# Batch norm rows over 128 partitions instead of 97 in a four-layer scan, convolution and attention kernel

## The chip, the cores and the metric

The kernel runs on one core of a Trainium2 chip. The metric is the device time of one execution in microseconds (us). TensorE is PE in the profile, VectorE is DVE, ScalarE is ACT, GpSimd is POOL, and SyncE is SP; SP computes nothing here and issues every DMA, in order, on one queue.

## What is computed

The input is x, of shape (4, 96, 64, 64): four images with 96 channels. Four layers follow each other. Layer 0 is a selective scan in four directions over the 4096 positions of an image, and it holds most of the work. Layer 1 is a block of three convolutions with batch norms (96 to 576 channels, 3x3 depthwise, 576 to 96). Layer 2 is a Fourier attention and a quantised feed-forward net; layer 3 is a linear attention and another such net. What bears on the change are two batch norms that follow a matrix product directly:

```python
# layer 1: h has 576 channels
scale = g * rsqrt(v + EPS);  shift = b - m * g * rsqrt(v + EPS)
h = relu(einsum('oc,bchw->bohw', w1, x) * scale + shift)
...
# layer 2: h has 192 channels
h = einsum('bnc,hc->bnh', x, w1)
h = relu((h - mean) * (gamma / sqrt(var + EPS)) + beta)
```

Scale and shift depend on weights alone. So the scale can be multiplied into the columns of the weight matrix, and the shift can become one more row of it, which is multiplied by a row of ones.

## The kernel before

**The folded matrices.** The kernel holds w1 as a matrix of 128 rows (input channels) by 576 columns, of which 96 rows are weights and row 96 is the shift; the tile wa1 of layer 2 is the same with 192 columns. The image has a channel 96 that is constant one. The generator `later_weights` (L324) builds them, once in the whole program. It loads each of the four batch norm vectors g, b, m, v as a row that is repeated over the partitions: `load_row` (L161) issues one DMA on SP whose source is the vector in DRAM, broadcast over as many partitions as the target has. The targets have C + 1 = 97 partitions (L332, L333 for layer 1, 576 columns; L382, L383 for layer 2, 192 columns). Then `rsqrt` (L167, L168, two ACT instructions) and three DVE instructions (L361, L363, L365, and L409, L410, L412) make scale and shift on all 97 partitions. Rows 0 to 95 of the scale multiply the weights (L367, L413), and row 96 of the shift is copied into row 96 of the matrix (L368, L415).

**The scan.** The long part of the program is `scans` (L1225). It walks through 1536 units, each one a block of 128 partitions by 1024 positions. For each unit ACT computes the decay (L1279), POOL multiplies the input by B (L1272), DVE runs the scan (L1286), DVE or POOL multiplies by C (L1301), and PE sums with a constant matrix (L1324). ACT is one unit ahead of the scan and POOL two. The inputs scan_d, scan_g, scan_B, scan_C are fetched by SP (L1257), each as a 512 KB load that is broadcast over partitions.

**What sets the order.** The instruction order of every engine is fixed when the program is built: the scan runs in a manual schedule, and after each unit a planner (`advance`) puts in steps of the other layers, which are written as generators that yield (engine, estimated time). The first stage that the planner serves is `weights` (L1219): `later_weights` beside `group_norm` of images 1 to 3 (L509). A group norm loads an image in eight chunks of 192 KB (`fetch_image`, L502) and takes the statistics of each chunk on DVE (`bn_stats`, L516). Both generators start together. So SP's queue holds, in this order: the loads of w1, w2 and other weights (L327), two of wout (L330, L331), the four rows of 576 columns and two of 96 columns (L162), then the first three chunks of image 1 (L502), then scan inputs (L1257), then the next chunks.

SP's DMAs take turns on eight semaphore lanes. A DMA waits at the head of SP's queue until the DMA eight before it has landed. The third chunk of image 1 is eight behind the first row, the next scan_g is eight behind the second, and so on.

The four layer-2 rows (L383) come about 110 us later in the same way, between the layer's other weights and two loads of rdid (L385, L386).

Of the kernel before, what the change touches and what calls it, by code (L numbers as in the profile page):

```python
# [27 lines left out]
B, C, H, W = 4, 96, 64, 64  # L28
L = H * W
K, NS, R, DI = 4, 16, 6, 192  # L30
NE = R + 2 * NS
HID, NT1 = 576, 5
# [64 lines left out]
def hybrid_kernel(ctx: ExitStack, tc: tile.TileContext, a: dict):  # L97
# [63 lines left out]
    def load_row(out, name):  # L161
        load(out, a["rows"][:, ROW[name]].partition_broadcast(out.shape[0]))  # L162
        return out
# [32 lines left out]
    def big(name):  # L196
        if last_room and turns(thirds) == "last":
            return last_room[0].tile([128, 6144], F32, name=name, tag="big", bufs=1)
        return bp.tile([128, 6144], F32, name=name, tag="big", bufs=2)
# [86 lines left out]
    def scratch(t):  # L286

        at = 0

        def take(parts, *shape):  # L290
            nonlocal at
            n = int(np.prod(shape))
            at += n
            out = t[:parts, at - n : at]
            return out if len(shape) == 1 else out.rearrange("p (a b) -> p a b", b=shape[1])

        return take
# [26 lines left out]
    def later_weights():  # L324
# [3 lines left out]
        take = scratch(big("weights"))  # L328
        wo_a, wo_b = take(128, C), take(64, C)
        load(wo_a, a["wout_t"][0:128])  # L330
        load(wo_b, a["wout_t"][128:DI])  # L331
        s1, t1 = take(C + 1, HID), take(C + 1, HID)  # L332
        g1, b1, m1, v1 = (load_row(take(C + 1, HID), n) for n in ("g1", "b1", "m1", "v1"))  # L333
        g2r, v2r = load_row(take(128, C), "g2"), load_row(take(128, C), "v2")
        yield wait(4)
        yield pe(1.0, 1)
# [40 lines left out]
        take = scratch(big("weights"))  # L377
# [1 line left out]
        load(pre, a["pre"])  # L379
        w1t = take(C, DI)  # L380
        load(w1t, a["wa1_t"])
        sa, ta = take(C + 1, DI), take(C + 1, DI)  # L382
        ga, ba, ma, va = (load_row(take(C + 1, DI), n) for n in ("bn1_g", "bn1_b", "bn1_m", "bn1_v"))  # L383
        g, v = load_row(take(128, C), "bn2_g"), load_row(take(128, C), "bn2_v")
        load_row(rdid[0:64], "rd")  # L385
        load_row(rdid[64:128], "id")  # L386
# [3 lines left out]
        n = 2 * NG  # L390
# [35 lines left out]
        take = scratch(big("weights"))  # L426
# [789 lines left out]
    def plan():  # L1216

        stats = (group_norm(b, arriving(b)) for b in range(1, B))
        out = [Stage("weights", 2, later_weights(), *stats)] + front(1) + front(2)  # L1219
        out += middle(0) + layers_2_and_3(0) + front(3)  # L1220
        for b in (1, 2):
            out += middle(b) + layers_2_and_3(b)
        return out
# [417 lines left out]
```

## Time and profile before

| what | value |
|---|---|
| time, median of 3 runs | 6271.16 us (6259.06 to 6287.62) |
| the profiled execution | 6292.35 us, of which the span is 6290.6 us |
| busy: PE, DVE, ACT, POOL | 74%, 86%, 61%, 81% of the span |
| DMA | 1078.10 MB, 171 GB/s on average |
| L1286, DVE scan, mean of one | 2.28 to 2.35 us by form |
| L1301, DVE product, mean of one | 1.225 us |
| L1272, POOL product, mean of one | 2.373 us |
| L516, DVE statistics of one chunk, median | 0.672 us |
| granted PE clock, mean | 0.837 |

Times in the profile are from the start of the span. A row of the timeline gives the start and the length in us, the engine, the line, the operation, what is written and read, and how many instructions were merged; in brackets stands how long the engine had been idle before and which event ended that. SPq rows are DMA issues on SP's queue. Their length is the time that the issue kept the queue, not that of the transfer.

### The profile page before, as it was taken

To read this page: it belongs to the slowest core of one execution; us is meant where nothing else is said; L and a number is where in the kernel's file an instruction comes from. 1 tells how busy PE (TensorE), PEld (TensorE's weight loads), DVE (VectorE), ACT (ScalarE), POOL (GpSimd) and SP (SyncE) were. 2 spreads that over 40 slices of the span, in tenths; PEclk is the share of its full clock that TensorE was granted. 3 is DMA by queue.
4 is the path that set the end of the run, shared out by engine and by line. 5 is a ranking of instruction groups with operands and counts; after the bars stand their busy time and mean duration, and the time that the engine had idled before them with its cause. 6 is when DMAs were issued, how large, how long until landed. Compare 5 with 4: busy or idle time off the path is not lost. (4 is left out here: it accounts for less than half of the span.)

```text
span 6290.6 us, 78721 instructions
## 1 busy us (share of the span) xinstructions
PE 4637.2 (74%) x27628; PEld 1718.8 (27%) x27628; DVE 5400.7 (86%) x3627; ACT 3837.2 (61%) x6056; POOL 5073.3 (81%) x2183
## 2 busy tenths in 40 slices
PE   6632867755887776686568887767888677778998
PEld 2100212211222542121112236321222542112283
DVE  4979898999999889989999998898999998899045
ACT  5743776764664576767545656767666567665334
POOL 4856878889999888888899998898999888899000
PEclk9855978877998888788679988778999888788999
DMA  5654565667644554456776446447754454674201
GB/s 184 215 159 139 188 203 186 215 212 231 205 155 144 179 181 140 139 192 194 226 228 188 157 147 202 154 156 220 228 162 156 165 176 156 188 223 139 72 15 37
DMA packets 424720, 1078.10 MB, mean 171 GB/s; under 512 B 79258, under 2 KB 81024, under 8 KB 423172
## 3 DMA queue, kind: packets, MB, share of 16 engines
q1 hardware_dynamic: 424324, 1073.06, 53.2%
q8 instruction: 220, 3.60, 0.2%
q14 instruction: 176, 1.44, 0.1%
HBM read 856.64 MB, written 220.66 MB: 171 GB/s over the span
## 5 line engine op out<-in xcount | busy, mean ns | idle before, releaser
L1272 POOL TENSOR_TENSOR scan_w<-scan_g,scan_B 128x1024 f32<-128x1024 f32 x1536 | 3606.6, 2373 | 452.8 <-PE ps_y L1324 358.3
L1279 ACT ACTIVATE ps_da<-scan_d,aneg 128x1024 f32<-128x1024 f32 x1536 | 1715.5, 1117 | 533.5 <-DVE scan_w L1286 273.6
L1301 POOL TENSOR_TENSOR scan_w<-scan_w,scan_C 128x1024 f32<-128x1024 f32 x640 | 1516.3, 2369 | 285.9 <-ACT state L1298 175.6
L1286 DVE TENSOR_TENSOR_SCAN ps_da<-ps_da,state,scan_w 128x1024 f32<-128x1024 f32 x672 | 1575.9, 2345 | 197.9 <-ACT ps_da L1279 175.1
L1324 PE MATMUL ps_y<-scan_w,cst 128*32 128x512 f32 x6144 | 1005.4, 733 | 561.6 <-ACT yt L1338 207.4
L1301 DVE TENSOR_TENSOR scan_w<-ps_da,scan_C 128x1024 f32<-128x1024 f32 x896 | 1097.3, 1225 | 71.6 <-DMA scan_C<-bc 3.6
L1286 DVE TENSOR_TENSOR_SCAN scan_w<-ps_da,state,scan_w 128x1024 f32<-128x1024 f32 x480 | 1123.4, 2340 | 38.8 <-ACT ps_da L1279 33.4
L1286 DVE TENSOR_TENSOR_SCAN ps_da<-ps_da,scan_w 128x1024 f32<-128x1024 f32 x224 | 511.9, 2285 | 86.3 <-ACT ps_da L1279 67.0
L1324 PEld LDWEIGHTS ps_y<-scan_w,cst 128*32 128x32 f32 x6144 | 148.4, 118 | 1215.6 <-issue 633.3
L1298 ACT COPY state<-ps_da 128x1 f32<-128x1 f32 x672 | 107.0, 159 | 603.4 <-DVE scan_w L1301 601.5
L1286 DVE TENSOR_TENSOR_SCAN scan_w<-ps_da,scan_w 128x1024 f32<-128x1024 f32 x160 | 364.8, 2280 | 23.9 <-ACT ps_da L1279 17.4
L827 PE MATMUL ps_mm<-h,wd 128*32 128x512 f32 x3168 | 366.5, 593 | 8.1 <-ACT r L167 7.0
L565 PE MATMUL ps_mm<-xp,taps 128*128 128x512 f32 x576 | 289.8, 646 | 62.3 <-ACT xp L545 31.0
L804 PE MATMUL ps_mm<-wd,w 128*32 128x512 f32 x2008 | 253.6, 616 | 20.7 <-ACT h L808 8.7
L616 PE MATMUL ps_mm<-xd,dtw 128*128 128x512 f32 x256 | 169.8, 756 | 99.6 <-ACT z L638 58.3
L999 PE MATMUL ps_mm<-wa,xp 128*64 128x96 f32 x1728 | 135.0, 319 | 99.4 <-DVE d L1004 80.5
L886 PE MATMUL ps_mm<-r,cst 128*128 128x512 f32 x220 | 152.0, 779 | 55.4 <-ACT acc L909 19.5
L625 ACT ACTIVATE z<-ps_mm 128x512 f32<-128x512 f32 x192 | 114.2, 595 | 127.9 <-PE ps_mm L620 62.1
L631 DVE SCALAR_TENSOR_TENSOR ps_mm<-ps_mm,z 128x512 f32<-128x512 f32 x192 | 131.7, 686 | 69.9 <-ACT z L629 69.0
L670 PE MATMUL ps_mm<-ya,cst 128*64 128x512 f32 x192 | 182.9, 1042 | 7.7 <-ACT acc L909 7.7
L1298 ACT COPY state<-scan_w 128x1 f32<-128x1 f32 x480 | 89.8, 187 | 152.1 <-DVE scan_w L1286 151.0
L808 ACT ACTIVATE h<-ps_mm 128x512 f32<-128x512 f32 x265 | 153.5, 595 | 46.0 <-PE ps_mm L804 43.7
(348 smaller groups left out, 6662.4 us busy)
## 6 DMA issues: line engine op xcount, KB each, us to landing
scan_g<-du SPq DMA_DIRECT2D x384, 512.0 KB, 5.1
scan_d<-delta SPq DMA_DIRECT2D x384, 512.0 KB, 6.0
scan_B<-bc SPq DMA_DIRECT2D x256, 512.0 KB, 5.0
scan_C<-bc SPq DMA_DIRECT2D x256, 512.0 KB, 5.4
y<-yt SPq DMA_DIRECT2D x384, 128.0 KB, 2.5
du<-g SPq DMA_DIRECT2D x128, 256.0 KB, 2.4
delta<-z SPq DMA_DIRECT2D x128, 256.0 KB, 2.7
tab<-in_etab SPq DMA_DIRECT2D x112, 256.0 KB, 4.3
```

The lines of the kernel that those rows point to most:

```text
L565: mm(p, lhsT=taps[:, t, 0:128], rhs=window(t, c + e), start=t == 0, stop=t == 8)
L616: mm(p, lhsT=dtw[:, o + 2 * third, 0:128], rhs=xd, start=True, stop=True)
L670: mm(split(p[:64]), lhsT=const("two")[:, :64], rhs=t[:, :L].rearrange("p (w h) -> p h w", h=H)[:, c * RPC : (c + 1) * RPC, :], start=True, ...
L804: mm(p[32 * n : 32 * n + 32], lhsT=w1[:, 32 * g : 32 * g + 32], rhs=xin[:, n : n + 15 : 2, 1 : W + 1], start=True, stop=True)
L808: act(h[:, :, 1 : W + 1], split(p), AF.Relu)
L827: mm(p[32 * n : 32 * n + 32], lhsT=held["wd"][:, groups[i], o, dx, :], rhs=here[i][:, :, dx : dx + W], start=dx == 0, stop=dx == 2)
L1272: nc.gpsimd.tensor_mul(x["w"], x["step"]["g"][x["i"]], x["step"]["B"][x["j"]])
L1279: act(x["da"], x["step"]["d"][x["i"]], AF.Exp, scale=aneg[:, av : av + 1])
L1286: nc.vector.tensor_tensor_scan(x["h"][:, order], x["da"][:, order], x["w"][:, order], start, ALU.mult, ALU.add)
L1298: nc.scalar.copy(step["last"][:, u : u + 1], x["h"][:, end : end + 1])
L1301: x["made"] = engine.tensor_mul(x["w"], x["h"], x["step"]["C"][x["j"]])
L1324: done = mm(y[32 * q : 32 * q + 32], lhsT=const("stack"), rhs=group[m]["w"][:, e * CH : e * CH + CH], start=first, stop=last)
```

## The change

The targets of the eight row loads, and the two pairs of tiles that the batch norms are computed in, have 128 partitions instead of 97. The ten instructions on them run over 128 partitions. The instructions of every engine, their order and the semaphores that they wait for are otherwise the same. Partitions 97 to 127 of scale and shift are read by nothing. The rows all lie in a scratch tile of 128 partitions, so that no other tile moves.

```diff
@@ later_weights
-        s1, t1 = take(C + 1, HID), take(C + 1, HID)
-        g1, b1, m1, v1 = (load_row(take(C + 1, HID), n) for n in ("g1", "b1", "m1", "v1"))
+        s1, t1 = take(128, HID), take(128, HID)
+        g1, b1, m1, v1 = (load_row(take(128, HID), n) for n in ("g1", "b1", "m1", "v1"))
...
-        sa, ta = take(C + 1, DI), take(C + 1, DI)
-        ga, ba, ma, va = (load_row(take(C + 1, DI), n) for n in ("bn1_g", "bn1_b", "bn1_m", "bn1_v"))
+        sa, ta = take(128, DI), take(128, DI)
+        ga, ba, ma, va = (load_row(take(128, DI), n) for n in ("bn1_g", "bn1_b", "bn1_m", "bn1_v"))
```

## The prediction

> **What bounds the kernel now.** I read first the page's busy shares: DVE 86%, POOL 81%, PE 74%, no engine near its limit over the whole span. That says nothing of a change that touches 18 instructions, so I went to the place of the change. The list of DVE's waits, over the whole span, has this near its top:
>
> ```profile
> DVE st L516 <- DMA x<-in_x: 57.0, 4, 37.3
> ```
>
> Four waits for an image chunk hold 57.0 us, one alone 37.3 us, the bulk. DVE's timeline shows where it is:
>
> ```profile
> 391.76 2.34 DVE L1286 TENSOR_TENSOR_SCAN scan_w<-ps_da,state,scan_w 128x1024 f32<-128x1024 f32 x1
> 431.36 1.88 DVE L516 BATCH_NORM_STATS2 st<-x 96x6 f32<-96x512 f32 x3 [37.25 <-DMA x<-in_x]
> 433.15 2.34 DVE L1286 TENSOR_TENSOR_SCAN ps_da<-ps_da,state,scan_w 128x1024 f32<-128x1024 f32 x1
> 435.58 1.22 DVE L1301 TENSOR_TENSOR scan_w<-ps_da,scan_C 128x1024 f32<-128x1024 f32 x1
> 438.89 1.28 DVE L516 BATCH_NORM_STATS2 st<-x 96x6 f32<-96x512 f32 x2 [2.08 <-DMA x<-in_x]
> ```
>
> From 394.1 to 431.36 DVE does nothing, with the scans queued behind the statistics. POOL and ACT run out of work too (POOL then waits 41.4 us for a scan on DVE). Why are the chunks late? SP's timeline of the same stretch:
>
> ```profile
> 390.42 0.50 SPq L331 DMA_DIRECT2D weights<-in_wout_t  x1
> 391.03 29.75 SPq L162 DMA_DIRECT2D weights<-in_rows  x6
> 420.83 1.89 SPq L502 DMA_DIRECT2D x<-in_x  x3
> 423.07 0.58 SPq L1257 DMA_DIRECT2D scan_g<-du  x1
> 423.70 0.59 SPq L1257 DMA_DIRECT2D scan_d<-delta  x1
> 430.63 0.51 SPq L1257 DMA_DIRECT2D scan_C<-bc  x1
> ```
>
> The six row issues keep SP for 29.75 us (the first two take 0.41 and 0.55 us, the slowest 9.53), and the chunks stand behind them. The DMA view of 395 to 421 us says what the engines do meanwhile:
>
> ```profile
> GB/s 28 21 25 25 25 25 21 28 11 18 11 25 28 25 25 25 28 25 25 28 25 25 25 25 25 25 25 25 25 25 28 25 25 25 25 46 56 43 25 25
> DMA packets 412, 0.68 MB, mean 26 GB/s; under 512 B 138, under 2 KB 138, under 8 KB 412
> ```
>
> A flat 25 GB/s, with the 16 engines 7.4% busy together, about one of sixteen. So a 97-row load runs on one DMA engine: 97 x 2304 B = 223.5 KB at 25 GB/s is 8.9 us, and four are 35.8 us, which is the stall. From 502 us the layer-2 rows do it again on a smaller scale:
>
> ```profile
> 502.08 13.70 SPq L162 DMA_DIRECT2D weights<-in_rows  x6
> ```
>
> **The change, part by part.** *The ten computing instructions* get 31 more partitions. Neighbouring rows price that: L365 over 97x576 took 0.75 us, L371 over 128x576 took 0.76 us, both TENSOR_TENSOR on DVE. Ten times 0.01 us is 0.1 us of DVE and ACT at most. I take 0.
>
> *The bytes* grow by 4 x 31 x 2304 B + 4 x 31 x 768 B = 0.38 MB. At the 320 GB/s that the DMA view shows for 20 to 26 us that is 1.2 us of the DMA engines, of which 0.9 us belong to the first group; below it is within the landing times.
>
> *The issue and transfer of the layer-1 rows* is the point. Do 128 rows spread over the engines? The same helper line broadcasts taps, 128 rows of 6912 B, at 20.6 us: the issue took 0.33 us, and from 20 to 26 us, with that load in the queue, the engines moved 320 GB/s at a busy share above 100% of sixteen. That row speaks for a full spread. The Trainium skill (DMA: Bandwidth & Descriptors, "Why a DMA increments its semaphore by 16 and not by 1") gives the cause: a copy uses the largest number up to 16 that divides the slowest dimension, hence one engine for 97 and sixteen for 128. The same page has a formula that speaks against the change ("Anatomy of one DMA", fitted on GpSimd's path): 2.0 us plus bytes over 436 GB/s. By it a row load is an estimated 2.5 us before and 2.7 us after, so that the change would cost 0.8 us over the four big loads and remove no stall. The rows say 8.9 us for one, so the trace decides against the formula for 97 rows; it may hold for 128.
>
> Now DVE's path after the change. Six issues at 0.6 us (the first two stand 0.72 us apart, the two of rdid take 1.16 us together) occupy SP from 391.03 to 394.6. The three chunks follow at 394.6, 395.2 and 395.8. How soon they land is what the trace of before can't show. The nearest row is the group of eight chunks of image 3, whose first three are issued at 526.15: these took 6.5 us each, with DMA saturated (349 GB/s from 524 to 534 us), and the eight have a median of 3.7. With 3.7 us the third lands at 399.5 and its statistics end at 400.2. With 6.5 us, at 402.3 and 403.0. Before, they ended at 433.24. So 30.2 to 33.0 us go; I take 31.8, a little nearer the median, since DMA is far from saturated there (80 GB/s from 391 to 393 us).
>
> The second wait, 2.08 us at 438.89, is for the fourth chunk. Today it stands behind scan_C, which waited 6.3 us for a row of its lane. After the change the rows land by about 397 to 400 us, that chunk is issued by 400.5 and lands by 407 at worst, against a need at 403.8 to 406.6 (3.6 us of scan and product after the third). I take the 2.08 us as gone; in the worst case 0.4 us of it stays. Together 31.8 + 2.1 = 33.9 us, from 31.9 to 35.1.
>
> What is late next? Behind the chunks SP issues scan_g, scan_d, scan_C. They move forward by as much as the chunks, and their tiles are used later; no engine waits for them today once DVE is going. I cost this at 0; with no cover one such load would cost its 5 to 7 us landing.
>
> *The layer-2 rows.* SP gets back about 13.70 - 3.6 = 10 us. Who waits for that? From 500 to 600 us DVE is busy 98.5 of 100 us, and POOL waits 1.5 us for scan_B, once, beside a busy DVE. That cover hides it: I take 0, with 0 to 2 us as the bound. Without it, up to 10 us would go.
>
> *Does the gain last?* The order on each engine is fixed and no step is tied to absolute time; after 442 us DVE is busy 59.3 of 60 us. What starts 34 us earlier there ends earlier, so the shift reaches the end.
>
> Sum: 6292.35 - 34 = 6258 us for the profiled execution; applied to the median, 6271.16 - 34 = 6237 us, or -0.54%.
>
> **The rivals.**
>
> *A smaller gain, the wait moves.* The chunks come early, but DVE then waits for a scan input or a chunk that is eight behind a row on its lane. For it: SP does wait on rows today (6.3 us), and x three is tied to row one. Against it: spread over sixteen engines a row needs 295 KB at 320 GB/s, 0.9 us. If half of the stall returned, the gain is 17 us: 6254 us. Chance 0.14.
>
> *No gain, a hidden stall.* PE, ACT and POOL would have to have been the bound elsewhere, so that DVE's lead is eaten up. For it: POOL is at 81%, and DVE waits 242.1 us in all for ACT's decays. Against it: POOL and ACT stand still in this stretch too. That gives 6271 us. Chance 0.06.
>
> *The rows don't spread.* If a broadcast of 128 rows stays on one engine, the big loads take 128/97 as long: 31/97 x 35.8 = 11.4 us more stall, plus up to 31/97 x 13.70 = 4.4 us at the second group, which DVE's backlog partly covers. The time is then 6283 to 6287 us, slower than before. The point that decides it is whether one DMA engine's 25 GB/s stays in force for the layer-1 rows. The taps row speaks against it. Chance 0.05.
>
> *The likeliest*, 0.75: the stall goes as summed, 32 to 37 us with the layer-2 bound, 6234 to 6239 us.
>
> **How the numbers follow.** About 0.5% is what a measurement of this kernel can tell from no change; that is 31.4 us, at the edge of the likeliest case. With the three runs before spread over 28 us, I give 0.55 of its 0.75 to a measured gain above it and the rest to a gain below it. Faster by over 0.5%: 0.55. Within: 0.42 (0.19 of the likeliest, 0.14, 0.06, and 0.03 of the unspread rows). Slower: 0.03 (0.02 of the unspread rows with an unlucky run, 0.01 of the likeliest for the same reason). The range 6222 to 6256 us takes in the bounds of the likeliest, the smaller gain, and about 14 us of run-to-run spread below.
>
> **What would show it.** In the profile after: the six row issues of layer 1 take 3 to 5 us in all instead of 29.75; no stretch of flat 25 GB/s; the wait of L516 for x falls from 37.25 to 4 to 8 us, and the 2.08 us wait goes; the layer-2 group falls from 13.70 to about 4 us with DVE as full as before; L361 to L365 and L167 keep their times to within contention; what follows comes some 34 us earlier and stays so. I am wrong if the row issues stay at several us each, if DVE has a new wait between 394 and 420 us, or if the shift shrinks on the way to the end.

## The result and the profile after

The changed kernel took 6252.83 us (median of 7 runs, 6243.48 to 6263.54) against 6276.19 us of the kernel before (median of 7, 6259.06 to 6290.77). The ratio is 0.9961, with a 95% interval of 0.9944 to 0.9978. A second comparison, made later, gave 6251.30 against 6285.86 us, 0.9938 (0.9917 to 0.9959). The forecast was 6237 us or 0.9946, with a range of 6222 to 6256. Both intervals contain 0.9946. The first measurement lies within 0.5% of no change, the second beyond it. The kernel before had medians from 6274.57 to 6285.86 us in the later comparisons, so each ratio below is to runs of it that were taken beside the kernel in question.

The profile after answers line by line. SP's timeline at the layer-1 rows:

```profile
391.04 2.97 SPq L162 DMA_DIRECT2D weights<-in_rows  x6
394.05 1.37 SPq L502 DMA_DIRECT2D x<-in_x  x3
395.77 0.57 SPq L1257 DMA_DIRECT2D scan_g<-du  x1
396.39 0.59 SPq L1257 DMA_DIRECT2D scan_d<-delta  x1
397.53 0.51 SPq L1257 DMA_DIRECT2D scan_C<-bc  x1
398.75 0.51 SPq L1257 DMA_DIRECT2D scan_d<-delta  x1
399.91 9.31 SPq L502 DMA_DIRECT2D x<-in_x  x5
```

Six issues take 2.97 us instead of 29.75, and the chunks stand in the queue 27 us earlier. The DMA view of 395 to 421 us, where a flat 25 GB/s stood:

```profile
GB/s 308 325 127 105 78 171 388 306 271 265 359 422 441 422 403 407 384 258 274 249 142 44 16 221 154 208 321 158 32 13 186 208 123 365 309 214 353 189 57 13
DMA packets 2566, 6.04 MB, mean 232 GB/s; under 512 B 591, under 2 KB 591, under 8 KB 2564
```

Nine times the bytes move in the same 26 us, nearly all of the difference being the chunks and scan inputs that had been stuck. DVE's timeline:

```profile
393.26 2.34 DVE L1286 TENSOR_TENSOR_SCAN scan_w<-ps_da,state,scan_w 128x1024 f32<-128x1024 f32 x1
400.57 2.14 DVE L516 BATCH_NORM_STATS2 st<-x 96x6 f32<-96x512 f32 x3 [4.97 <-DMA x<-in_x]
402.63 2.34 DVE L1286 TENSOR_TENSOR_SCAN ps_da<-ps_da,state,scan_w 128x1024 f32<-128x1024 f32 x1
405.06 1.22 DVE L1301 TENSOR_TENSOR scan_w<-ps_da,scan_C 128x1024 f32<-128x1024 f32 x1
408.19 1.28 DVE L516 BATCH_NORM_STATS2 st<-x 96x6 f32<-96x512 f32 x2 [1.91 <-DMA x<-in_x]
```

The two waits are 4.97 and 1.91 us instead of 37.25 and 2.08: 32.45 us are gone.

The profiled execution took 6243.48 us, 48.9 us less than the profiled one of before. That is more than the stall. Where does it come from? DVE runs 1536 scans in the same order in nearly every kernel here, so I lined up the two traces scan by scan and took how much earlier or later each scan starts. This is worked out from the traces. The shift is counted from scan 73, the last before the stall (at 391.76 us in the profile of before), to scan 101, some 170 us later, and then to the last scan.

| kernel | shift at scan 101, us | at the last scan, us |
|---|---|---|
| after | -30.9 | -45.3 |
| after, second trace | -28.2 | -43.0 |
| before, second trace | +0.3 | -0.9 |
| layer-1 rows only | -32.3 | -43.2 |
| layer-2 rows only | -0.7 | -15.1 |
| 127 partitions | +14.3 | -3.0 |
| 98 partitions | -30.0 | -52.5 |
| compute on 97 | -30.4 | -48.4 |
| 97, statistics later | -19.0 | -54.8 |
| 128, statistics later | -33.6 | -40.2 |
| 128, statistics later, one load | -38.2 | -46.3 |
| 128, one load | -30.2 | -35.1 |

The stall is the first column. What comes after it is spread: the layer-2-only kernel keeps the stall and still ends 15.1 us before the profile of before. The first column is read for causes, the ratios of many runs for the total. Differences of about 2 us in it mean little: SP issues the first row 0.7 to 2.3 us before scan 73 starts, by the trace, and the wait is shorter by as much. Counted from the first row issue to the first statistics, so without this lead, the time is 40.3 to 40.7 us in the three traces with 97 rows in layer 1 (both of before, layer 2 only) and 9.5 to 9.9 us in the four with 128 and the old order (both of after, layer 1 only, compute on 97), about 31 us less.

### The profile page after: what moved, and what is told of

It reads as the page before. It is cut to its first block, busy times and chain, and to the rows that moved or that the text cites. A ratio compares the mean times of both kernels' runs of the same rounds, so it can differ in the third digit from the quotient of the medians.

```text
span 6241.7 us, 78721 instructions
## 1 busy us (share of the span) xinstructions
PE 4613.8 (74%) x27628; PEld 1708.1 (27%) x27628; DVE 5389.0 (86%) x3627; ACT 3836.7 (61%) x6056; POOL 5072.1 (81%) x2183
## 5 line engine op out<-in xcount | busy, mean ns | idle before, releaser
L808 ACT ACTIVATE h<-ps_mm 128x512 f32<-128x512 f32 x265 | 153.5, 595 | 46.3 <-PE ps_mm L804 43.6
L565 PEld LDWEIGHTS ps_mm<-xp,taps 128*128 128x128 f32 x576 | 115.6, 208 | 237.9 <-issue 160.4
```

Of the source, the lines that this page charges most:

```text
L565: mm(p, lhsT=taps[:, t, 0:128], rhs=window(t, c + e), start=t == 0, stop=t == 8)
L808: act(h[:, :, 1 : W + 1], split(p), AF.Relu)
```

## The experiments

The theory: a 97-row load runs on one DMA engine, because 97 has no divisor that splits it; the four large ones hold that engine for some 36 us and SP for nearly 30, and DVE stands behind a chunk of image 1 in SP's queue. The rivals: the full width of 128 counts, in the load or in the computing; all eight loads share in the gain; or the gain is given back.

**One half of the change at a time.** First the layer-1 rows alone:

```diff
-        s1, t1 = take(C + 1, HID), take(C + 1, HID)
-        g1, b1, m1, v1 = (load_row(take(C + 1, HID), n) for n in ("g1", "b1", "m1", "v1"))
+        s1, t1 = take(128, HID), take(128, HID)
+        g1, b1, m1, v1 = (load_row(take(128, HID), n) for n in ("g1", "b1", "m1", "v1"))
```

> Only the layer-1 rows (576 columns) get 128 partitions, the layer-2 rows stay at 97. Theory (the stall near 394 us comes from four 97-row loads that each run on one DMA engine): all of the gain is here, the wait of L516 falls from 37.3 us to about 5 us, the scans behind it come 32 us earlier, time about 0.995 of before; the layer-2 issues stay at about 13.7 us. Rival (the gain is made by all eight loads, in proportion to their bytes or issue times, 29.75 to 13.70): 22 us earlier, 0.9965.

Measured: 0.9946 (0.9927 to 0.9965). SP and DVE in its timeline:

```profile
389.53 2.95 SPq L162 DMA_DIRECT2D weights<-in_rows  x6
470.02 14.40 SPq L162 DMA_DIRECT2D weights<-in_rows  x6
...
399.04 2.12 DVE L516 BATCH_NORM_STATS2 st<-x 96x6 f32<-96x512 f32 x3 [4.85 <-DMA x<-in_x]
406.69 1.31 DVE L516 BATCH_NORM_STATS2 st<-x 96x6 f32<-96x512 f32 x2 [1.96 <-DMA x<-in_x]
```

The layer-1 wait has fallen to 4.85 us with the layer-2 issues still at 14.40 us. Then the layer-2 rows alone (the other two lines of the diff, 97 kept in layer 1):

> Only the layer-2 rows (192 columns) get 128 partitions, the layer-1 rows stay at 97. Theory: the layer-2 issues fall from 13.7 to about 4 us but nobody waits, so the scans move by 0 to 2 us and the time is 0.999 to 1.001 of before; the wait of L516 stays at 37.3 us. Rival (proportional): 10 us earlier, 0.998.

Measured: 1.0001 (0.9989 to 1.0014, 14 runs).

```profile
389.85 29.72 SPq L162 DMA_DIRECT2D weights<-in_rows  x6
500.56 5.73 SPq L162 DMA_DIRECT2D weights<-in_rows  x6
...
430.32 1.88 DVE L516 BATCH_NORM_STATS2 st<-x 96x6 f32<-96x512 f32 x3 [35.93 <-DMA x<-in_x]
```

SP is relieved by 8 us in the second group (the issues take 5.73 us, not the expected 4), and DVE had not been waiting for it. The whole gain belongs to the layer-1 rows, and the proportional rival falls.

**What about 97?** `C + 1` becomes 127 in all eight loads and in the tiles that they are computed in:

```diff
-        s1, t1 = take(C + 1, HID), take(C + 1, HID)
+        s1, t1 = take(127, HID), take(127, HID)
...
```

> All eight rows get 127 partitions, a prime. Theory (number of engines is a divisor of the partitions): still one engine at 25 GB/s, the layer-1 loads take 127/97 of 35.8 us, so the wait of L516 grows by about 11 us to 48 us and the kernel is slower by 11 to 13 us, 1.002. Rival (97 is bad for being few or for ending inside a block of 32 partitions, and more partitions are better): nearly all of the gain, 0.995.

Measured: 1.0020 (1.0009 to 1.0030, 22 runs). More partitions made it slower. SP, DVE and POOL:

```profile
394.03 40.41 SPq L162 DMA_DIRECT2D weights<-in_rows  x6
516.15 18.68 SPq L162 DMA_DIRECT2D weights<-in_rows  x6
...
445.20 1.88 DVE L516 BATCH_NORM_STATS2 st<-x 96x6 f32<-96x512 f32 x3 [47.70 <-DMA x<-in_x]
...
543.44 2.35 POOL L1272 TENSOR_TENSOR scan_w<-scan_g,scan_B 128x1024 f32<-128x1024 f32 x1 [6.76 <-DMA scan_B<-bc]
```

The layer-1 issues grow by 10.7 us and the wait by 10.5 us, close to 30/97 of 35.8 us, or 11.1. The second group, hidden at 97, shows here: POOL waits 6.76 us for scan_B, and by scan 101 another 4.2 us are lost. So its cover in the kernel before was nearly used up.

Then 98, by the same edit with 98 in place of 127:

> All eight rows get 98 partitions, one more than before; 98 is 14 times 7. Theory: 14 engines share each load, 7 rows each, so a layer-1 load takes about 0.7 us instead of 8.9, the wait of L516 falls to 5 us and the time is as with 128 partitions, 0.995. Rival (full 128 partitions are what counts): no gain, 1.000.

Measured: 0.9954 (0.9933 to 0.9975).

```profile
391.95 2.76 SPq L162 DMA_DIRECT2D weights<-in_rows  x6
...
400.79 0.69 DVE L516 BATCH_NORM_STATS2 st<-x 96x6 f32<-96x512 f32 x1 [5.58 <-DMA x<-in_x]
```

One partition more than before takes 27 us off SP. The full width isn't what counts; it is whether the count can be divided among the DMA engines. This is the rule of the Trainium skill that the prediction used ("Why a DMA increments its semaphore by 16 and not by 1"): by it 97 and 127 go to one engine, 98 to fourteen, 128 to sixteen. The four counts behave as it says. How many engines a load used can be counted in the DMA line of each profile's page, here of before, 127, 98 and after, in this order:

```profile
DMA packets 424720, 1078.10 MB, mean 171 GB/s; under 512 B 79258, under 2 KB 81024, under 8 KB 423172
DMA packets 424960, 1078.47 MB, mean 171 GB/s; under 512 B 79258, under 2 KB 81144, under 8 KB 423412
DMA packets 424832, 1078.12 MB, mean 173 GB/s; under 512 B 79362, under 2 KB 81132, under 8 KB 423284
DMA packets 425088, 1078.48 MB, mean 173 GB/s; under 512 B 79378, under 2 KB 81268, under 8 KB 423540
```

The data of the eight rows moves in packets of 2304 and 768 B, so it isn't in the count under 512 B. That count is the same for 97 and 127, 104 higher for 98 and 120 higher for 128. For each of the eight loads that is 13 and 15 more, as one small packet per engine would make it: one engine, fourteen, sixteen. Layer 1 alone and layer 2 alone, four loads each, have 60 more.

**The computing.** The loads are as in the changed kernel, and the ten instructions run on 97 partitions:

```diff
-        nc.vector.tensor_mul(s1, s1, g1)
+        nc.vector.tensor_mul(s1[: C + 1], s1[: C + 1], g1[: C + 1])
...
```

> Loads as in the changed kernel (128 partitions), but the ten instructions that compute scale and shift run on 97 partitions as before. Theory: as the changed kernel, 0.995 to 0.996 of before, L361 to L365 with the same lengths, so the computing has no part in it. Rival (the partitions computed matter): the gain is visibly smaller or larger than 31 us at the stall.

Measured: 0.9946 (0.9926 to 0.9967), shift -30.4 against -30.9 and -28.2 us of the two traces of the changed kernel. L361, L363 and L365 take 1.91, 2.78 and 0.75 us as in the changed kernel. The computing has no part in it.

**What is late next, if DVE doesn't wait for the chunk?** The kernel before, with the statistics of image 1 twelve units later in the order:

```diff
-                yield wait(2)
+                yield wait(14 if b == 1 else 2)
```

> Rows at 97 partitions as before, but the statistics of image 1 are placed 12 units later in the order, so that DVE isn't held by an image chunk while the rows load. It tells what is late next. Theory: SP and one DMA engine are still held for 30 us and more, and scan_C, which is fetched only some three units before its product, is queued behind the rows; the wait moves there and DVE still stands for 20 to 32 us before 440 us: 0.997 to 1.000. Rival (the chunks alone hold the scan, scan inputs have cover enough): the stall is gone, about 0.994.

Measured: 0.9942 (0.9922 to 0.9963), though SP and the DMA engine were held as before:

```profile
411.67 2.32 DVE L1286 TENSOR_TENSOR_SCAN ps_da<-ps_da,state,scan_w 128x1024 f32<-128x1024 f32 x1
437.65 1.23 DVE L1301 TENSOR_TENSOR scan_w<-ps_da,scan_C 128x1024 f32<-128x1024 f32 x1 [23.66 <-DMA scan_C<-bc]
...
392.48 29.69 SPq L162 DMA_DIRECT2D weights<-in_rows  x6
```

On the wait the theory holds: DVE ran on until 414 us and then stood 23.66 us, for scan_C, which is queued behind the rows. So the scan inputs have about 20 us of cover, less than the 30 us for which the rows hold SP. On the time it doesn't: the ratio is that of the full gain. This edit changes the planner's order to the end of the program (the first and last shift, -19.0 and -54.8 us, differ more than in any other kernel), so the total mixes the stall with a new order. What the new order gained, and where, stays open.

**The rest of the wait.** The changed kernel, with the statistics two units later:

```diff
-                yield wait(2)
+                yield wait(4 if b == 1 else 2)
```

> The changed kernel, and the statistics of image 1 two units later in the order, to hide what is left of the wait (4.97 and 1.91 us). Theory: the landing of a chunk in 7 to 8 us is then covered, the waits of L516 for x in this place go, and the kernel is 6 to 7 us faster than the changed one: 0.994 of before. Rival (the next input is late by as much): no gain over the changed kernel, 0.9955.

Measured: 0.9945 (0.9925 to 0.9965).

```profile
403.66 0.69 DVE L516 BATCH_NORM_STATS2 st<-x 96x6 f32<-96x512 f32 x1 [0.93 <-DMA x<-in_x]
404.79 1.28 DVE L516 BATCH_NORM_STATS2 st<-x 96x6 f32<-96x512 f32 x2 [0.44 <-DMA x<-in_x]
414.17 0.69 DVE L516 BATCH_NORM_STATS2 st<-x 96x6 f32<-96x512 f32 x1 [3.08 <-DMA x<-in_x]
```

The first wait fell to 0.93 us, but a later chunk was late instead (3.08 us), and the waits for x from 391 to 480 us sum to 6.7 us, against 6.9 in the changed kernel. The wait moved, as the rival said. Next, in addition, the four vectors of a batch norm come in one load, since they lie side by side in DRAM:

```diff
-        g1, b1, m1, v1 = (load_row(take(128, HID), n) for n in ("g1", "b1", "m1", "v1"))
+        four = take(128, 4, HID)
+        load(four, a["rows"][:, ROW["g1"].start : ROW["v1"].stop].partition_broadcast(128))
+        g1, b1, m1, v1 = (four[:, i] for i in range(4))
```

> As the kernel before it, and the four rows of a batch norm, which lie side by side in DRAM, come in one load of 128 partitions instead of four. SP saves six issues. Theory: SP has no waiters there any more, so the time is the same within 2 us as without this edit, 0.994 of before. Rival (issues on SP still cost): 2 to 4 us less again.

Measured: 0.9934 (0.9916 to 0.9951), 6242.89 us, shift -38.2 us. The waits for x are down to this (L520 is L516 of the other kernels):

```profile
401.47 0.69 DVE L520 BATCH_NORM_STATS2 st<-x 96x6 f32<-96x512 f32 x1 [0.28 <-DMA x<-in_x]
409.13 0.69 DVE L520 BATCH_NORM_STATS2 st<-x 96x6 f32<-96x512 f32 x1 [0.89 <-DMA x<-in_x]
```

And the one load without the later statistics:

> The changed kernel with the four rows of a batch norm in one load of 128 partitions, and the order of the statistics as in the changed kernel. It parts the two edits of the fastest kernel so far. Theory: the three chunks are issued about 2 us earlier and the wait of L516 falls from 4.97 to about 3 us; 2 to 4 us faster than the changed kernel at the stall. Rival (only both edits together help): as the changed kernel, 32 us before the scans of the kernel before.

Measured: 0.9950 (0.9934 to 0.9966), shift -30.2 us, first wait 5.34 us. The wait is no shorter than in the changed kernel, and the theory's 2 to 4 us didn't come. About 1 us is gained all the same, hidden by the lead of SP: the chunks were issued 1.6 us after the first row instead of 3.0, and the first statistics started 8.5 us after it instead of 9.5; but the first row went out only 0.9 us before scan 73 here, against 2.2 us in the first trace of the changed kernel. Both edits together are 7.3 us ahead of the changed kernel at scan 101, which is more than the 4.6 us that separate them from the later statistics alone. Their totals don't tell them from the changed kernel, as the intervals overlap; by the traces it is the fastest version at this place.

**Second traces.** The kernel before, unchanged:

> The kernel before, unchanged, for a second trace. Theory (the 49 us between the two profiled spans hold some 15 us that are spread from run to run, since the layer-2-only kernel also ends 15 us before that profile): its scans keep within 2 us of the first trace up to 550 us from the start and end 5 to 20 us earlier. Rival (the change also speeds the later scans): it ends within 5 us of the first trace.

Measured: 1.0004 (0.9987 to 1.0022). The wait was 36.77 us, and the last scan came 0.9 us earlier than in the first trace. The theory's 5 to 20 us didn't come. The rival's number came, but the rival doesn't follow: the kernels that keep the stall, layer-2 only and 127, gained 14.4 and 17.3 us between scan 101 and the last. Why both traces of the unchanged program are slower there isn't settled. The granted PE clock moves with it: 0.837 and 0.838 in these two traces, 0.840 and 0.841 in those two. Over the 37 runs of the kernel before that were taken beside the first four experiments, the longer ones have the lower clock (correlation -0.60, about 2.8 us for each 0.001), which makes an estimate of 6 to 11 us of the difference; whether the clock is its cause wasn't tried. The changed kernel, unchanged:

> The changed kernel, unchanged, for a second trace and more runs. Theory: 32 us at the stall again, and with more runs a ratio of 0.9945 to 0.996, since 31 of 6275 us is 0.9951. Rival (part of the gain is given back later): at the stall 32 us, and a ratio above 0.9965.

Measured: 0.9938 (0.9917 to 0.9959); the first wait was 5.97 us, and the shift -28.2 us. Neither expected ratio was met exactly. Apart from 1.2 us (see the layer-2 rows below), nothing points to a gain that is given back. The five comparisons of kernels with spread rows, single loads and the old order (0.9961, 0.9938, 0.9946, 0.9954, 0.9946) have a plain mean of 0.9949, which is 32 us of 6276.

## Why the prediction was right

*The stall and its cause* held. Single halves, 98 and 127 show that it is the number of engines that a row load of layer 1 can use. The engine's backlog counts besides SP's queue: in before, the first chunk was issued at 420.83 and landed 10.5 us later, at 431.33, with the DMA at 22 to 26 GB/s from 429.1 us on; in the changed kernel it took 6.5 us. The estimate of 2.7 us for a load of 128 rows was not met as a landing time (the third and fourth took 4.2 and 4.8 us, with other loads in flight), and the 0.8 us worked out from it for four loads is 0.7 when summed unrounded.

*The size of the first wait.* The prediction took 31.8 us off the end of the third statistics. The first row went out at the same time in both traces (391.03 and 391.04 us), and that end moved from 433.24 to 402.71, so by 30.5 us. Two terms were off, in opposite directions: the issues took 2.97 us, not 3.6, and the traced landings of the chunks took 6.5 to 8.3 us (median 7.2), not 3.7 to 6.5. That the wait itself lost 32.28 us, so near to 31.8, is luck: DVE came to scan 73 1.5 us later in this trace, and had been 1.8 us later at the first scan, long before any row. Why the chunks landed so late is shown in part. While the fourth to sixth were on the way, the other loads that had been stuck moved too (359 to 441 GB/s from 401.5 to 406 us in the view above). But from 396.3 to 398.9 us, with the first one on the way, the rate was 78 to 171 GB/s, so heavy traffic alone doesn't explain its 6.5 us, and that stays open.

*The second wait* was a step that failed. The prediction let the 2.08 us go, since the fourth chunk would land by 407 us. It was issued at 399.91, as foreseen, but took 8.3 us, and 1.91 us stayed; so the two waits lost 32.45 us, not 33.9. The worst case of 0.4 us had joined the latest landing with the latest need.

*The layer-2 rows* were costed at 0, with a gain as the only bound. Their issues fell to 5.64 us, not to 4, and they cost 1.2 us in the trace: from scan 89 to scan 93 the shift, counted here from the first scan, goes from -32.4 to -31.2 us, and in the layer-2-only kernel from -2.1 to -0.9, while with layer 1 alone it stays at -33.0. The first L395 in that stretch took 1.35 us before and takes 2.60 us after:

```profile
492.73 2.35 POOL L1272 TENSOR_TENSOR scan_w<-scan_g,scan_B 128x1024 f32<-128x1024 f32 x1 [0.18 <-PE ps_y L1324]
493.69 2.60 DVE L395 TENSOR_TENSOR weights<-cst,weights 128x1152 f32<-128x1152 f32 x1
```

With layer 1 alone it is short again, and there POOL's next product had still waited for scan_B behind the layer-2 rows:

```profile
492.19 1.35 DVE L395 TENSOR_TENSOR weights<-cst,weights 128x1152 f32<-128x1152 f32 x1
...
493.55 2.34 POOL L1272 TENSOR_TENSOR scan_w<-scan_g,scan_B 128x1024 f32<-128x1024 f32 x1 [2.52 <-DMA scan_B<-bc]
```

The thirteen traces hold 39 of these L395. Five started while POOL waited for scan_B (both traces of before, layer 1 only, 127, and 97 with the statistics later); they took 1.35 us. The other 34 started beside a running POOL product and ended 1.21 to 1.22 us after that product did, so they took 1.55 to 3.51 us. Above, the product ends at 495.08 and L395 at 496.29. So L395 seems to wait until the product has ended. In the first trace of before the product came second, at 524.77, and it was the one that took longer, 3.15 us. The relief of POOL let its product start first. This is read from the traces; no experiment moved POOL's product alone.

*Nothing late next* held for the changed kernel, but the reason given, that the tiles are used later, had less room than it sounds: the later statistics show that scan_C has 20 us.

*The gain lasts*: in the two traces of the changed kernel it is 32.2 and 29.5 us at once, 30.9 and 28.2 by scan 101, where the 1.2 us of L395 are gone, and 32 us in the mean of the totals.

*The rivals.* The rows did spread; the 127-partition kernel shows what the rival on the slower side would have looked like, and its price was about right: 11.4 us of added stall were forecast for unspread 128, and 127 measured 10.5, plus 4.2 us at the second group. The hidden stall didn't occur. Of the wait that moves, 6.88 us stayed, not half of the stall. The likeliest outcome, a gain of about 0.54%, was at the edge of what can be told from no change; the first measurement fell below 0.5% and the second above.

## What to carry to other kernels

Look for loads in the trace during which the DMA rate is flat at one engine's pace, here 25 GB/s, and check whether the partition count can be divided: one row more, 98 for 97, was worth as much as 31 more. A load of 0.2 MB on one engine isn't only slow itself: all that is queued behind it on the issuing engine waits too, and the wait shows at an instruction that has nothing to do with it. Before a wait is costed as gone, price the landing of the load behind it too: 6.5 to 8.3 us here, where loads of the same size elsewhere had a median of 3.7.

## What the hardware did that was not expected

An issue on SP can be long. The third to sixth row issue took 3.36 to 9.53 us each while one DMA engine was behind, and the six took 0.33 to 0.58 us each when the rows were spread, so the queue of issues itself was held up. And with POOL freed of a wait, one DVE instruction took 1.9 times as long, 2.60 for 1.35 us: in 34 of 34 cases it ended 1.2 us after the POOL product that had started before it. So a relief off the critical path cost 1.2 us on it.
